# A two-layer decoder on one core: the first group's rows and weight quads ahead of the other groups' rows, and the next group's first quad ahead of its attention

## The chip, the cores and the metric

The kernel runs on one core of a Trainium2 chip, as one launch. The metric is device time in microseconds (us), as the median of several executions. Before the change it is 1839.93 us (three executions, 1838.93 to 1842.21). The engines are named as in the profile: PE is TensorE (matrix products and transposes), PEld its weight loads, DVE is VectorE, ACT is ScalarE, POOL is GpSimd, SP is the engine that issues most of the transfers.

## The reference, cut to what matters

`x` is (16, 128, 256) float32: 16 sequences of 128 rows of width 256. Two layers of three blocks each, every block followed by a residual sum and a layer norm:

```
x = LN(x + causal attention, 16 heads of 64)                     number 0
x = LN(x + 8 dense experts, gated by ctx_512 and itok)            number 1
x = LN(x + 2 shared and 16 routed experts, top 2)                 number 2
x = LN(x + attention with a band of 8, 16 heads of 16)            number 3
x = LN(x + cross attention to ctx_512, 16 heads of 16)            number 4
x = LN(x + 8 GELU experts, weighted by a top-1 gate)              number 5
```

For block 1 the gate of expert e at a key position is the sum over r of `ctx_512` where `itok` equals e. Everything is computed in float32.

## The kernel before, in words

**Tiling.** The 16 sequences form NG = 4 groups of GB = 4 sequences, so a group is 512 rows. Its rows are the tile `x` (128 partitions, 4 x 256), and their transpose is `xT` (128 partitions, 2 x 512), made by `transposed` from eight PE transposes (line 51) and two copies, one on DVE (244) and one on ACT (246).

**Attention 0** (`attention0`, from line 347) walks through four quads of four heads. `load_quad` (87) is four transfers of 256 KB: the columns of W_Q, W_K, W_V and the rows of W_O. The tile has three buffers (pool `attn`). `project_quad(j)` makes qT, kT and v of the quad: for i = 0, 1 two products of 512 columns for q and two for k (`project`, 288), evicted by DVE (361) and by ACT (366), then `values` (298): two PSUM tiles of four products of 256 columns (305), each evicted by a DVE copy (309). All of these, the transposes of x and the output products share the two buffers of the PSUM tag "H". A unit (j, b) is one quad for one of the group's four sequences: scores (382) into the single buffer "S", then `softmax` (313): minimum with the causal mask on DVE (319), maximum on DVE (324), four exponentials on ACT (329), reciprocal on DVE (334), product on POOL (335); two steps later the transposes of the weights (51) with an ACT copy (344), two more steps later the product with v (424) and its eviction zT (431), a step later the output product (391) and its sum into x (264). While the units n = 0 to 11 run, each step also takes one piece of `project_quad(j + 1)`. The group's quad 0 is projected by itself, ahead of its unit 0, and during its last four units and the five steps of draining nothing is projected.

**Gates of block 1.** `gates0` (731) reads `it` and `cx` (lines 734 and 293; one buffer each), makes eight tiles `chose` on DVE (743, four buffers shared with `sums`), sums each over the partitions with a product with ones (752), copies the sums on ACT (757), and stores them to HBM (759). They are read back as `gt` (768). It is called from `tail(0, g)`, after attention 0 of the group.

**Order of the work.** `Weaver.weave` fixes the program order at build time: it takes the pieces of a main stream, of a side stream `dense` and of short streams in turn, by a clock of estimated durations; `yield UNTIL` holds a stream until a time of that clock. The attention blocks of groups 0 and 1 are woven alone, those of groups 2 and 3 with `dense` (blocks 1, 2 and 5 of all groups), by shares of 81 to 150; then blocks 3 and 4 with the rest of `dense` (68 to 150); then the rest of `dense` alone. The framework's scheduler then orders each engine's instructions, which can put an instruction far ahead of its place in the program: the first four `chose` of group 0 stand at the very beginning of DVE's stream. In the trace each of DVE, ACT, POOL and SP runs its instructions in the order of its stream. SP's stream is its queue of transfers, with eight semaphores in turn, so that a transfer is issued only once the eighth before it has landed.

**The prologue.** Lines 106 to 108 issue the rows of group 0, quad 0, and the rows of groups 1 to 3; quads 1 and 2 follow, then `it`, `cx`, and weights of block 1. Four short streams `tail(-1, g)` (line 1008) transpose all groups' rows ahead of the first projection.

Of the kernel before, what the change touches and what calls it, by code (L numbers as in the profile page):

```python
# [14 lines left out]
P = 128  # L15
# [4 lines left out]
NG = NB // GB  # L20
# [7 lines left out]
def kernel(ctx: ExitStack, tc: tile.TileContext, a: dict, out: bass.AP):  # L28
# [15 lines left out]
    def bank(tag):  # L44
        return ps.tile([P, T], F32, tag=tag, name=f"ps{tag}")

    mm = nc.tensor.matmul
# [15 lines left out]
    def load_x(g):  # L63
        x = xp.tile([P, GB, D], F32, tag="x", name="x")
        nc.sync.dma_start(
            out=x, in_=a["x"][g * GB:(g + 1) * GB].rearrange("b p d -> p b d")
        )
        return x

    def load_w(tag, size, name, *parts, bufs=None):  # L70
        w = (ap if tag == "attn" else wp).tile([P, size], F32, tag=tag, name=name, bufs=bufs)
        views, at = [], 0
        for part in parts:
            p_, r, c = part.shape
            v = w[:, at:at + r * c].rearrange("p (r c) -> p r c", r=r)
            nc.sync.dma_start(out=v, in_=part)
            views.append(v)
            at += r * c
        return views
# [7 lines left out]
    def load_quad(j):  # L87

        cols = slice(j * D, (j + 1) * D)
        return load_w(  # L90
            "attn", 2048, f"wquad{j}", a["L0_attn_W_Q"][:, :, cols], a["L0_attn_W_K"][:, :, cols],
            a["L0_attn_W_V"][:, :, cols], a["L0_attn_W_O"][:, 2 * j:2 * j + 2, :],
        )
# [9 lines left out]
            f"wg{t}", a["L0_ffn_wg_r"][:, :, cols], a["L0_ffn_wu_r"][:, :, cols]  # L103
        ) + load_down(f"wd{t}", a["L0_ffn_wd_r"][:, 2 * t - 2:2 * t, :])

    xs = [load_x(0)]
    first_quad = load_quad(0)
    xs += [load_x(g) for g in range(1, NG)]


    ident = cp.tile([P, P], F32, tag="ident", name="ident")
    make_identity(nc, ident)
    ones = cp.tile([P, P], F32, tag="ones", name="ones")
    nc.gpsimd.memset(ones, 1.0)
    mhalf = cp.tile([P, GB], F32, tag="mhalf", name="mhalf")
    nc.gpsimd.memset(mhalf, -0.5)

# [66 lines left out]
    UNTIL = "until"  # L184
# [47 lines left out]
    weaver = Weaver()  # L232
# [52 lines left out]
    def project(pt, w, cols, xT):  # L285

        for c in range(KC):
            mm(pt, lhsT=w[:, c, cols], rhs=xT[:, c, :], start=c == 0, stop=c == KC - 1)  # L288
# [9 lines left out]
    def values(xT, w, k):  # L298

        v = p3.tile([P, GB, D], F32, tag="v", name="v")  # L300
        for b in range(0, GB, 2):
            pv = bank("H").rearrange("p (b f) -> p b f", b=2)
            for i in range(2):
                for c in range(k):
                    mm(  # L305
                        pv[:, i, :], lhsT=xT[:, c, (b + i) * P:(b + i + 1) * P],
                        rhs=w[:, c, :], start=c == 0, stop=c == k - 1,
                    )
            nc.vector.tensor_copy(v[:, b:b + 2, :], pv)
            yield 0.86 * k  # L310
        return v
# [32 lines left out]
        return eT, nc.scalar.copy(eT, pt)  # L344


    def attention0(x, xT, g):
        norm = Norm(x)
        norm.bias(bo0)
        heads = {}  # L350

        def project_quad(j):
            wq, wk, wv, wo = first_quad if g == 0 and j == 0 else load_quad(j)
            qT = p2.tile([P, 2, T], F32, tag="qT", name="qT")
            kT = p2.tile([P, 2, T], F32, tag="kT", name="kT")
            for i in range(2):
                c = 2 * j + i
                cols = slice(i * P, (i + 1) * P)
                pq = bank("H")
                project(pq, wq, cols, xT)  # L360
                nc.vector.tensor_scalar(
                    qT[:, i, :], pq, bq0[:, c:c + 1], 0.125, ALU.add, ALU.mult
                )
                pk = bank("H")
                project(pk, wk, cols, xT)
                nc.scalar.activation(kT[:, i, :], pk, AF.Identity, bias=bk0[:, c:c + 1])
                yield 3.44

            v = yield from values(xT, wv, KC)
            heads[j] = qT, kT, v, wo  # L370

        def scores(j, b):
            qT, kT, _, _ = heads[j]
            at = slice(b * P, (b + 1) * P)
            s = ps.tile([P, 2, T], F32, tag="S", name="psS", bufs=1)[:, :, :D].rearrange(
                "p s (i k) -> p s i k", i=2
            )

            for i in range(2):
                for k in range(2):  # L380
                    rows = slice(64 * k, 64 * k + 64)
                    mm(  # L382
                        s[:, k, i, :], lhsT=qT[rows, i, at], rhs=kT[rows, i, at],
                        start=True, stop=True,
                    )
            return softmax(s, causal)

        def output(j, b, zT):
            po = bank("H")[:, :D]
            for i in range(2):  # L390
                mm(po, lhsT=zT[:, i, :], rhs=heads[j][3][:, i, :], start=i == 0, stop=i == 1)  # L391
            norm.add(b, po, last=j == 3)

        yield from project_quad(0)
        units = [(j, b) for j in range(4) for b in range(GB)]
        e, eT, zT, at = {}, {}, {}, {}
        for n in range(len(units) + 5):
            if n < 16:
                j, b = units[n]
                e[n] = scores(j, b)  # L400
                at["e", n] = weaver.now + 9.0
                yield 0.6
            m = n - 2
            if m in e:
                yield UNTIL, at["e", m]
                eT[m], _ = weights_T(e.pop(m))
                at["t", m] = weaver.now + 2.5
                yield 0.5
            m = n - 5
            if m in zT:  # L410
                yield UNTIL, at["z", m]
                output(*units[m], zT.pop(m))
                yield 0.86
            m = n - 4
            if m in eT:
                j, b = units[m]
                yield UNTIL, at["t", m]

                pz = bank("O")[:, :D].rearrange("p (c q) -> p c q", c=2)
                got = eT.pop(m)  # L420
                for i in range(2):
                    for k in range(2):
                        h = 2 * i + k
                        mm(  # L424
                            pz[64 * k:64 * k + 64, i, :],
                            lhsT=heads[j][2][:, b, 64 * h:64 * h + 64], rhs=got[:, 2 * k + i, :],
                            start=True, stop=True,
                        )
                zT[m] = p3.tile([P, 2, P], F32, tag="z", name="zT")

                nc.vector.tensor_tensor(
                    zT[m], pz, bv0[:, 2 * j:2 * j + 2].unsqueeze(2).to_broadcast([P, 2, P]), ALU.add
                )
                at["z", m] = weaver.now + 2.5
                yield 0.6
            if n < 12:

                j, b = units[n]
                if b == 0:
                    ahead = project_quad(j + 1)  # L440
                yield next(ahead)
                if b == 3:
                    assert next(ahead, None) is None
        assert not e and not eT and not zT
        norm.done()
# [498 lines left out]
        )  # L944


    xTs = [None] * NG
    written = [-1] * NG
    extra = [None] * NG

    def tail(number, g):

        if number >= 0:
            yield UNTIL, weaver.now + 7.0
        xTs[g], last = transposed(xs[g], xTs[g])
        transposed_by[g] = [last]
        yield 0.9
        if number == 0:
            yield from gates0(g)
        elif number in (1, 4):  # L960
            yield UNTIL, weaver.now + 2.5
            extra[g] = yield from (route if number == 1 else gate1)(xTs[g])
        written[g] = number
# [13 lines left out]
    def run(number, g):  # L977

        yield lambda: written[g] == number - 1
        x, xT = xs[g], xTs[g]  # L980
        if number == 0:
            yield from attention0(x, xT, g)
        elif number == 1:
            yield from ensemble0(x, xT, g)
        elif number == 2:
            yield from experts0(x, xT, extra[g])
        elif number == 3:
            yield from attention1(x, xT)
        elif number == 4:
            yield from cross1(x, xT, g)  # L990
        else:
            yield from experts1(x, xT, g, extra[g])
        if number not in (1, 5):
            after(tail(number, g))

    def chain(*layers):
        for layer in layers:
            yield from run(*layer)
# [6 lines left out]


    b2sum = cp.tile([P, D], F32, tag="b2sum", name="b2sum")
    weaver.short += [Stream(tail(-1, g)) for g in range(NG)]
    dense = Stream(chain(
        (1, 0), (1, 1), (2, 0), (2, 1), (1, 2), (1, 3), (2, 2), (2, 3),  # L1010
        (5, 0), (5, 1), (5, 2), (5, 3),
# [76 lines left out]
```

## Time and profile before

| what | value |
|---|---|
| median of 3 executions | 1839.93 us |
| the profiled execution | 1837.82 us |
| its span, first to last instruction | 1836.1 us |
| PE busy in the span | 1757.7 us (96%) |
| DVE, ACT, POOL busy | 1050.7, 731.0, 673.8 us |
| PE idle, 0 to 30 us | 12.7 us |
| ACT table loads | 113, of 1.28 us each |

The span counts from the first to the last instruction of the profiled execution; 1.7 us lie around it. A line of the timeline gives start, length, engine, source line, operation, output and inputs, the number of records, and in brackets the idle time before it with what ended it. A float32 product counts as two records. A line of the stages gives a stretch of time, its length, the busy time of each engine with the number of records, the granted TensorE clock, the share of the DMA engines and GB/s.

### The profile page before, as it was taken

What the parts mean: (1) busy time and instruction counts of PE and PEld (TensorE: products, weight loads), DVE (VectorE), ACT (ScalarE), POOL (GpSimd) and SP (SyncE); (2) the same over time, 40 slices, a digit from 0 to 9 for tenths busy, and PEclk for the clock granted to TensorE, in tenths of its full rate; (3) what the DMA queues carried; (4) which work ended last, traced back from release to release, by engine and by line L of the source; (5) the groups of instructions that cost most, each with busy time, mean ns of one, the idle gap of its engine ahead of it and who ended that gap; (6) DMA issues with size and microseconds to landing.
All of it is one profiled execution on the core that took longest, in us unless ns stands there. A gap on an engine that the chain in (4) does not pass through costs nothing.

```text
span 1836.1 us, 21774 instructions
## 1 busy us (share of the span) xinstructions
PE 1757.7 (96%) x7602; PEld 1068.6 (58%) x7602; DVE 1050.7 (57%) x1927; ACT 731.0 (40%) x2161; POOL 673.8 (37%) x568
## 2 busy tenths in 40 slices
PE   7999999999999999999899999999898999999997
PEld 4655566666566565556556565556554565555664
DVE  3555655677565244676776853356546555645645
ACT  2434312112023452151340544936827548376221
POOL 5231235422131222353432624456554234344222
PEclk9999999999999999999999999999998999999999
DMA  5041223323321324123223214232232121222221
GB/s 170 24 134 46 87 78 126 124 75 122 121 86 46 111 92 138 61 99 111 75 87 98 82 57 121 70 116 97 79 116 75 63 94 65 75 75 84 106 96 51
DMA packets 73404, 166.69 MB, mean 91 GB/s; under 512 B 7000, under 2 KB 38800, under 8 KB 73296
## 3 DMA queue, kind: packets, MB, share of 16 engines
q1 hardware_dynamic: 70464, 150.17, 25.5%
q0 software_dynamic: 2832, 15.15, 2.0%
q8 instruction: 60, 0.98, 0.2%
q14 instruction: 48, 0.39, 0.1%
HBM read 148.32 MB, written 16.97 MB: 90 GB/s over the span
## 4 chain that ended last, share of the span: by engine, by line
PE 74%; DVE 11%; ACT 8%; issue 3%; POOL 2%; DMA 2%; SPq 0%; POOLq 0%; DVEq 0%; ACTq 0%
PE psH L288 33%; PE psM L671 16%; ACT e L329 4%; PE psH L305 4%; PE psM L592 4%; PE psO L51 4%; PE psH L391 3%; DVE cm L663 3%; PE psS L382 2%; PE psS L465 2%; PE psO L424 2%; PE psO L477 2%; DVE nmax L324 1%; PE psH L51 1%; ACT L933 1%
## 5 line engine op out<-in xcount | busy, mean ns | idle before, releaser
L288 PE MATMUL psH<-xT,we 128*128 128x512 f32 x1024 | 488.6, 599 | 5.6 <-ACT h L933 3.6
L335 POOL TENSOR_TENSOR e<-e,inv 128x512 f32<-128x512 f32 (+1 forms) x128 | 190.0, 1484 | 420.2 <-DVE inv L334 376.4
L663 POOL TENSOR_TENSOR cm<-h 128x512 f32<-128x512 f32 x128 | 205.3, 1621 | 356.1 <-DVE h L774 164.6
L671 PE MATMUL psM<-cm,wb 128*128 128x256 f32 x1280 | 313.9, 385 | 2.1 <-DVE acc L681 1.6
L329 ACT ACTIVATE e<-e,nmax 128x128 f32<-128x128 f32 x512 | 198.6, 389 | 258.6 <-DVE nmax L324 258.2
L671 PEld LDWEIGHTS psM<-cm,wb 128*128 128x128 f32 x1280 | 238.5, 190 | 99.3 <-issue 65.4
L288 PEld LDWEIGHTS psH<-xT,we 128*128 128x128 f32 x1024 | 187.4, 190 | 165.9 <-issue 137.1
L663 DVE TENSOR_TENSOR cm<-h 128x512 f32<-128x512 f32 x192 | 219.2, 1165 | 40.3 <-ACT h L933 37.9
L681 DVE TENSOR_TENSOR acc<-psM,acc 128x512 f32<-128x512 f32 x224 | 138.5, 619 | 174.8 <-PE psM L671 174.2
L344 ACT COPY eT<-psO 128x512 f32<-128x512 f32 x192 | 106.7, 586 | 147.2 <-PE psO L51 146.3
L933 ACT ACTIVATE h<-psH,b 128x512 f32<-128x512 f32 x128 | 87.2, 687 | 186.1 <-PE psH L288 169.3
L774 DVE SCALAR_TENSOR_TENSOR h<-psH,gt 128x512 f32<-128x512 f32 x128 | 87.7, 685 | 80.4 <-PE psH L288 80.3
L671 PE MATMUL psM<-h,wb 128*128 128x256 f32 x512 | 124.3, 385 | 0.0
L288 PE MATMUL psH<-xT,wquad 128*128 128x512 f32 x256 | 118.7, 606 | 4.6 <-DMA wquad<-in_L_attn_W_Q 1.6
L671 PEld LDWEIGHTS psM<-h,wb 128*128 128x128 f32 x512 | 96.5, 192 | 32.8 <-issue 18.7
L288 PE MATMUL psH<-xT,wg 128*128 128x512 f32 x256 | 115.5, 594 | 0.0
L51 PEld LDWEIGHTS psO<-ident,e 128*128 128x128 f32 x768 | 87.3, 141 | 48.4 <-issue 29.5
L51 PE MATMUL psO<-ident,e 128*128 128x128 f32 x768 | 112.5, 280 | 1.7 <-POOL e L335 0.9
L329 ACT ACTIVATE e<-psS,nmax 128x128 f32<-128x128 f32 x256 | 89.9, 377 | 38.4 <-DVE nmax L324 35.4
L329 ACT ACTIVATION_READ_ACCUMULATOR e<-e,nmax 128x1 f32 x512 | 95.7, 187 | 0.0
L457 POOL TENSOR_TENSOR kb<-kT,hm 128x512 f32<-128x512 f32 x64 | 70.1, 1097 | 69.2 <-PE psS L465 33.2
L879 POOL TENSOR_TENSOR hT<-sg,cw 128x512 f32<-128x512 f32 x32 | 41.4, 1292 | 130.6 <-DVE sg L878 130.6
(173 smaller groups left out, 2243.8 us busy)
## 6 DMA issues: line engine op xcount, KB each, us to landing
wb<-wbd SPq DMA_DIRECT2D x48, 896.0 KB
we<-in_L_xattn_proj_in SPq DMA_DIRECT2D x32, 512.0 KB
we<-in_L_ffn_w SPq DMA_DIRECT2D x32, 512.0 KB
wbd<-wb POOLq DMA_DIRECT2D x16, 896.0 KB, 6.0
gt<-gatesd SPq DMA_DIRECT2D x32, 256.0 KB
cw<-combd SPq DMA_DIRECT2D x64, 128.0 KB
wquad<-in_L_attn_W_Q SPq DMA_DIRECT2D x16, 256.0 KB
wquad<-in_L_attn_W_K SPq DMA_DIRECT2D x16, 256.0 KB
```

Source lines behind the costliest of these rows:

```text
L51: return nc.tensor.transpose(out_, in_, ident[:n, :n])
L288: mm(pt, lhsT=w[:, c, cols], rhs=xT[:, c, :], start=c == 0, stop=c == KC - 1)
L305: mm(pv[:, i, :], lhsT=xT[:, c, (b + i) * P:(b + i + 1) * P], rhs=w[:, c, :], start=c == 0, stop=c == k - 1,)
L329: nc.scalar.activation(e[:, h, :], s[:, h // (n // 2), h % (n // 2), :], AF.Exp, bias=nmax[:, h:h + 1], accum_out=total[:, h:h + 1],)
L335: nc.gpsimd.tensor_tensor(e, e, inv.unsqueeze(2).to_broadcast([P, n, P]), ALU.mult)
L344: return eT, nc.scalar.copy(eT, pt)
L592: step = mm(acc[b], lhsT=held[:, b * P:(b + 1) * P], rhs=down(i), start=i == 0 and b % 2 == 0, stop=i == n - 1, skip_group_check=True,)
L663: engine.tensor_tensor(t[:, s % 2], half(e, one), half(e, two), op)
L671: step = mm(pm[:, s % 2, :], lhsT=blocks[e][:, s, q, :], rhs=parts[e, s][:, q, :], start=q == 0 and s % 2 == 0, stop=q == 1, skip_group_ch ...
L681: nc.vector.tensor_tensor(to, pm[:, :len(slots), :], to, ALU.add)
L774: nc.vector.scalar_tensor_tensor(out=h, in0=ph, scalar=0.0, in1=up[1], op0=ALU.max, op1=ALU.mult)
L933: nc.scalar.activation(h, ph, AF.Gelu, bias=b1[:, 4 * e + c:4 * e + c + 1])
```

## The change

- The rows of group 0 are followed by quads 0 and 1. The rows of groups 1 to 3 are issued by a new stream `begin(g)`, at 20 g us of the weaver's clock, and transposed ten of its microseconds later.
- Nine products of a tile of ones with itself are put on PE ahead of everything else.
- `project_quad` takes the group as well; during units 12 to 15 of groups 0, 1 and 2 it projects quad 0 of the next group, which then skips its own first projection. The table `heads0` is shared by the groups.

In the streams as built, SP's transfers up to `cx` are the same 18 (22 times 256 KB), in the order x0, quad 0, quad 1, x1, quad 2, x2, x3, it, cx. On DVE the first `chose` stands ahead of the first copy of v, and two more ahead of the second. The transposes of groups 1, 2 and 3 stand in group 0's attention, at units 5, 10 and 14. ACT has 105 table loads.

```diff
-    xs = [load_x(0)]
-    first_quad = load_quad(0)
-    xs += [load_x(g) for g in range(1, NG)]
+    xs = [load_x(0)] + [None] * (NG - 1)
+    first_quads = [load_quad(j) for j in range(2)]
...
     nc.gpsimd.memset(ones, 1.0)
+
+    pw = bank("M")
+    for _ in range(9):
+        mm(pw[:, :P], lhsT=ones, rhs=ones, start=True, stop=True)
...
-    def attention0(x, xT, g):
+    xTs = [None] * NG
+    heads0 = {}
+
+    def attention0(x, g):
         norm = Norm(x)
         norm.bias(bo0)
-        heads = {}
-
-        def project_quad(j):
-            wq, wk, wv, wo = first_quad if g == 0 and j == 0 else load_quad(j)
+
+        def project_quad(g, j):
+            wq, wk, wv, wo = first_quads[j] if g == 0 and j < 2 else load_quad(j)
+            xT = xTs[g]
...
             v = yield from values(xT, wv, KC)
-            heads[j] = qT, kT, v, wo
+            heads0[g, j] = qT, kT, v, wo
...
-        yield from project_quad(0)
+        if (g, 0) not in heads0:
+            yield from project_quad(g, 0)
...
-            if n < 12:
+            if n < 16 and (n < 12 or g + 1 < NG):
 
                 j, b = units[n]
                 if b == 0:
-                    ahead = project_quad(j + 1)
+                    ahead = project_quad(g, j + 1) if j < 3 else project_quad(g + 1, 0)
                 yield next(ahead)
...
-    weaver.short += [Stream(tail(-1, g)) for g in range(NG)]
+    def begin(g):
+
+        if g > 0:
+            yield UNTIL, 20.0 * g
+            xs[g] = load_x(g)
+            yield UNTIL, 20.0 * g + 10.0
+        yield from tail(-1, g)
+
+    weaver.short += [Stream(begin(g)) for g in range(NG)]
```

More of the change, by code (lines that the diff above doesn't have):

```diff
@@ L369, in project_quad @@
             v = yield from values(xT, wv, KC)
-            heads[j] = qT, kT, v, wo
+            heads0[g, j] = qT, kT, v, wo
         def scores(j, b):
-            qT, kT, _, _ = heads[j]
+            qT, kT, _, _ = heads0[g, j]
             at = slice(b * P, (b + 1) * P)
@@ L390, in output @@
             for i in range(2):
-                mm(po, lhsT=zT[:, i, :], rhs=heads[j][3][:, i, :], start=i == 0, stop=i == 1)
+                mm(po, lhsT=zT[:, i, :], rhs=heads0[g, j][3][:, i, :], start=i == 0, stop=i == 1)
             norm.add(b, po, last=j == 3)
-        yield from project_quad(0)
+        if (g, 0) not in heads0:
+            yield from project_quad(g, 0)
         units = [(j, b) for j in range(4) for b in range(GB)]
@@ L425, in attention0 @@
                             pz[64 * k:64 * k + 64, i, :],
-                            lhsT=heads[j][2][:, b, 64 * h:64 * h + 64], rhs=got[:, 2 * k + i, :],
+                            lhsT=heads0[g, j][2][:, b, 64 * h:64 * h + 64], rhs=got[:, 2 * k + i, :],
                             start=True, stop=True,
@@ L944, in experts1 @@
         )
-    xTs = [None] * NG
     written = [-1] * NG
@@ L981, in run @@
         if number == 0:
-            yield from attention0(x, xT, g)
+            yield from attention0(x, g)
         elif number == 1:
```

## Prediction

> **What bounds the kernel now.** I read the page first: busy shares and the chain that ended last.
>
> ```profile
> PE 1757.7 (96%) x7602; PEld 1068.6 (58%) x7602; DVE 1050.7 (57%) x1927; ACT 731.0 (40%) x2161; POOL 673.8 (37%) x568
> ...
> PE 74%; DVE 11%; ACT 8%; issue 3%; POOL 2%; DMA 2%; SPq 0%; POOLq 0%; DVEq 0%; ACTq 0%
> ```
>
> PE is the bound; all that can be won is its idle time, 1836.1 - 1757.7 = 78.4 us. The change works in the first 230 us, so I asked next for the stages there (columns: stretch, length, busy PE, PEld, DVE, ACT, POOL, granted clock, DMA share, GB/s):
>
> ```profile
> 18.05:31.25 13.20, 11.42 (x40) 6.43 (x40) 5.13 (x8) 1.65 (x3) 9.32 (x8) 1.00 0.69 231
> 31.25:71.00 39.75, 39.75 (x238) 24.91 (x236) 24.36 (x48) 22.27 (x84) 9.57 (x11) 1.00 0.03 10
> 98.67:126.71 28.04, 25.67 (x126) 15.54 (x125) 14.04 (x35) 6.31 (x21) 4.80 (x6) 1.00 0.37 118
> 126.71:150.00 23.29, 18.74 (x98) 10.14 (x98) 14.73 (x24) 9.64 (x35) 9.93 (x12) 0.93 0.38 119
> 200.00:229.50 29.50, 27.05 (x126) 14.12 (x124) 17.42 (x39) 5.09 (x14) 6.57 (x5) 1.00 0.32 99
> ```
>
> From 31 to 71 us PE has no idle time at all: what is moved in there costs its full length. Idle: 2.37 us where group 0 drains and group 1 starts, 4.55 in the stage of the gates, 2.45 from group 1 to 2. Then the timeline of DVE and PE at the two places where DVE holds PE up:
>
> ```profile
> 25.55 0.69 DVE L743 SCALAR_TENSOR_TENSOR chose<-it,cx 128x512 f32<-128x512 int32 x1 [4.73 <-DMA cx<-in_ctx]
> ...
> 143.21 0.69 DVE L743 SCALAR_TENSOR_TENSOR chose<-it,cx 128x512 f32<-128x512 int32 x1 [4.19 <-DMA cx<-in_ctx]
> ```
>
> ```profile
> 14.16 1.94 PE L51 MATMUL psH<-ident,x 128*128 128x128 f32 x8 [0.23 <-DMA x<-in_x]
> 16.63 1.07 PE L51 MATMUL psH<-ident,x 128*128 128x128 f32 x8 [0.53 <-DMA x<-in_x]
> 18.05 7.13 PE L288 MATMUL psH<-xT,wquad 128*128 128x512 f32 x16 [0.35 <-DVE xT L244]
> 26.96 3.72 PE L305 MATMUL psH<-wquad,xT 128*128 128x256 f32 x16 [1.78 <-DVE qT L361]
> ...
> 31.25 3.70 PE L288 MATMUL psH<-xT,wquad 128*128 128x512 f32 x8
> ...
> 144.62 0.71 PE L382 MATMUL psS<-kT,qT 64*128 64x128 f32 x8 [3.37 <-DVE e L319]
> ...
> 146.81 4.97 PE L288 MATMUL psH<-xT,wquad 128*128 128x512 f32 x8
> ```
>
> A `chose` of DVE waits for the transfer of `cx`, and what stands behind it in DVE's stream waits too: the second qT (26.16), so PE's products for v.
>
> **What the Trainium skill says.** "TensorE: Matmul & The Clock Gate", Part 1: a TensorE idle for a window of about 3.4 us falls to half clock and needs about as much activity to come back. The trace agrees: eight transposes take 1.94 us at 14.16 and 1.07 at 16.63; after the idle 3.37 us eight records take 4.97 in place of 3.70. The same page, Part 4, has it that transposes don't count as activity; here they warmed the array by 16.63, before any product. The same page, "Architectural detail", calls VectorE's queue a strict FIFO; the 4.73 us at 25.55, with a qT ready behind it, agree. "DMA: Bandwidth & Descriptors", section "Queues, rings and completion order": each DMA engine takes descriptors in ring order. So `cx` lands after what is issued ahead of it, whatever the order of that.
>
> **The change, part by part.**
>
> *1. The first projection moves forward, but cx does not.* x0 landed at 5.09; with 1.94 us of transposes, copies to 7.64 and 7.13 us of projection, PE ends quad 0's q and k near 15.3, v (3.72) near 19.0, scores at 19.7. The next product, q of quad 1, needs the bank of the first half of v. Its copy stands on DVE behind the first `chose`. `cx` is the 18th transfer, behind the same 5.5 MB as before, in a stretch where the DMA engines are 93% busy; I take 25.55 again (bounds 24.5 and 26.5). `chose` to 26.24, copy of v to 26.9: PE goes on there, where before it did at 31.25, 4.3 us earlier. It has been idle for over 7 us, so it resumes cold: 3.4 to 5 us at half clock lose 1.3 (as at 146.81) to 2.5; I take 1.9. Gain 2.4.
>
> *2. The nine products of ones.* They and the earlier start lie wholly ahead of 26.9, hidden behind the wait for `cx`: nothing either way. If that cover were gone, warm transposes would save 0.9 us (1.94 - 1.07).
>
> *3. 24 transposes leave the prologue*, where PE waited for rows anyway, for the full stretch from 31 us on. One group's eight displaced 0.53 + 0.58 us at 118.78 to 120.32: 3 x 1.1 = 3.3 us lost. Their two copies (0.69, 0.59) fit in DVE and ACT; three bias sums on POOL (9.26 / 4 = 2.3 us each) stand between weight products that have a step of slack. Parts 1 and 3: 0.9 us lost.
>
> *4. The next group's quad ahead.* At the end of group 0 the built stream has group 1's scores between the last output products, and quad 1's projection directly behind. Of the idle 2.37 us I leave 0.5 (the last zT, 0.53 at 107.26): gain 1.9. From group 1 to 2, of 2.45 leave 0.65: gain 1.8. From 2 to 3 the dense stream covers it already: 0. The price: the tile of the quad is released by the output products of unit n = 12, and the transfer must land at once. The same wait at quad 3 cost 0.35 us at 71.07 and 0.85 at 172 to 175; three more of them, with one covered by dense: 1.0 lost (0 to 2).
>
> *5. The gates' stage.* Count from the first product of the gates, T0 (126.71 before). SP: before, the stores of the sums waited 3.6 us behind a weight transfer (`we`, 131.63), gt was issued 3.9 us after the stores, `it` and `cx` at 137.41 and 138.17, and `cx` landed 5 us later, T0 + 16.5. In the built order `we` stands behind `cx`, so the stores come at T0 + 2, gt at 6, `cx` at 8.2, landing at 12.6 to 13.4. PE has work until T0 + 14.9: gates 2.1, four transposes of weights, v, scores, the projection's first half, an output, a q. Then k of the second half needs a bank that DVE's sum into x frees, behind `chose`, `chose`, e, `chose`, nmax and the sum: 4 x 0.69 + 0.67 + 0.4 = 3.8 us after landing, T0 + 16.4 to 17.2. Idle 1.5 to 2.3 us plus small ones, in place of 4.55 and the 1.27 of cold clock: gain 2.7 (bounds 0 and 4.5).
>
> *6. Later.* Quad 0 of group 2 leaves the stage that is woven with dense, so dense stands 11 us x 150/81 = 20 us later against the main stream from there on. The stream has 105 ACT table loads for 113, 8 x 1.28 = 10 us less of ACT, of which I put a tenth on the path: gain 1.0. The new neighbourhoods of the rest can cost or give some 3 us.
>
> **Sum**, against the profiled span: -2.4 + 3.3 - 1.9 - 1.8 + 1.0 - 2.7 - 1.0 = -5.5, 1836.1 to 1830.6, with the 1.7 us around it 1832.3. The profiled execution (1837.82) stood 2.1 under the median of 1839.93; so the median goes to 1834.4.
>
> **Rivals.**
>
> *Nothing to measure.* The wait for the second `cx` stays as long as before (a landing at T0 + 16.5 would put PE's return beyond T0 + 17.9, where it was), and only boundaries and transposes are left, which nearly cancel. For it: DVE's longer queue ahead of the bank's release; against it: `we` is out of the way on SP. Without part 5, and with 1.3 for part 6's neighbourhoods, 1834.4 + 2.7 + 1.3 = 1838.4.
>
> *Slower: ACT in layer 1.* From 1140 to 1500 us PE is idle for 17.2 us, in stretches where ACT switches between Exp and GELU tables and is full (19.82 of 20 us at 1300 to 1320). Moving dense by 20 us rearranges this. If eight more of the 1.28 us loads came to lie on the path there, in place of one less, PE would lose 10.2 us: 1834.4 + 10.2 = 1844.6. It decides once the exposed loads there grow by more than 7, which eats 9.2 us (5.5 and the 3.7 of the bound). Against it: for the two functions the built stream has 34 + 46 loads, before 35 + 50.
>
> *Far faster.* If `cx` landed 8 us earlier, quad 1 would follow quad 0 at once and part 1 would give some 10 us more: 1824. Against it: the chain shows W_K of quad 1 landing at 18.17 and `cx`, eight transfers of 256 KB later, at 25.55, which is 285 GB/s; at that rate the 5.5 MB alone take 19 us from their start.
>
> That the change doesn't do what it says is excluded by the built order, which I compared.
>
> **Numbers.** Forecast 0.60 (own range 1831.5 to 1837.5), nothing 0.22, slower 0.13, far faster 0.05. 0.2% is 3.7 us, about what a measurement of this kernel can tell from no change. Of the forecast 0.47 lies under 1836.2, 0.13 above; of "nothing" 0.02 under, 0.18 within, 0.02 above. Faster 0.54, same 0.31, slower 0.15. Range 1827 to 1842: it takes in the bounds of parts 1, 4, 5 and 6 and leaves out the far faster case and the worse two thirds of the slower one.
>
> **What would show it.** PE idle from about 19 to 27 us, ended by DVE's copy of v, DVE waiting until 25 or 26 for `cx`; products at half speed after it. Quad 1's k ended near 32.5 (before 34.95). Idle at the drains under 1 us. In the gates' stage one PE wait of about 2 us, ended by DVE's sum into x. PE busy within 3 us of 1757.7, its idle time 5 us less. I would be wrong if `cx` lands well before 24, if PE waits over 4 us in the gates' stage, or if idle from 1140 on changes by more than 4 us.

## The result, and the profile after

| kernel | median | against before (95%) |
|---|---|---|
| before, beside it | 1837.65 us (13 executions) | |
| changed | 1842.45 us (13 executions, 1839.51 to 1847.49) | 1.0028 (1.0020 to 1.0037) |

The change costs about 5 us; the forecast was a gain of 5.5. The medians below come from several series of executions, each with the kernel before beside it, and a ratio is against that one. The page of the changed kernel (busy time of each engine; the chain that ended last, by engine):

```profile
span 1840.9 us, 21821 instructions
...
PE 1768.8 (96%) x7620; PEld 1071.2 (58%) x7620; DVE 1046.8 (57%) x1927; ACT 721.7 (39%) x2153; POOL 674.1 (37%) x568
...
PE 77%; DVE 9%; ACT 7%; DMA 2%; issue 2%; POOL 1%; SPq 0%; POOLq 0%; DVEq 0%; ACTq 0%
```

PE's idle time fell, from 78.4 to 72.1 us, and the kernel is slower all the same: PE is busy 11.1 us longer. The ones are 4.0 of that; the other 7.1 are the same 7602 records taking longer. DVE and ACT have less to do than before. A page's sums don't say where the time went. So I gave each kind of PE record one length (0.43 us for 512 columns, 0.22 for 256, 0.13 for a transpose, and so on, from the groups of the page), added them up in the order of the built stream without the ones, and read from the timeline when each amount of work was reached. The difference to before is a kernel's lead (below zero) or lag at that point, in us:

| before is at | 46.7 | 161 | 269 | 707 | 1135 | 1271 | 1444 | 1591 | end |
|---|---|---|---|---|---|---|---|---|---|
| changed | -1.1 | -8.7 | -6.0 | -6.1 | -7.7 | +5.7 | -1.4 | +5.1 | +4.8 |

The early part does what was forecast of it, with a lead of 6.0 us after the boundary of groups 1 and 2. It is lost in layer 1, in two parts: 13.4 us where before goes from 1135 to 1271 (1127 to 1277 on the clock of the changed kernel), of which 7.1 come back by 1444, and 6.5 more by 1591. (Such a table is of one profiled execution. It shows the place of a loss better than its size: the profiled executions of e3 and e4 below ran 3.7 and 2.8 us over the medians of their kernels, and small differences between the rows can be the execution's. The lengths given to the records are a choice too; another such choice moves an entry by up to about 1 us.)

The early part in the timeline of the changed kernel, DVE and then PE (start, length, operation, idle time before it and what ended that):

```profile
24.05 0.69 DVE L750 SCALAR_TENSOR_TENSOR chose<-it,cx 128x512 f32<-128x512 int32 x1 [11.44 <-DMA cx<-in_ctx]
24.66 0.68 DVE L312 COPY v<-psH 128x512 f32<-128x512 f32 x1
...
143.65 1.30 DVE L750 SCALAR_TENSOR_TENSOR chose<-it,cx 128x512 f32<-128x512 int32 x2 [2.11 <-DMA cx<-in_ctx]
```

```profile
1.21 3.98 PE L117 MATMUL psM<-ones 128*128 128x128 f32 x18 [1.21 <-POOL ones L113]
5.03 1.04 PE L51 MATMUL psH<-ident,x 128*128 128x128 f32 x8
6.41 7.13 PE L291 MATMUL psH<-xT,wquad 128*128 128x512 f32 x16 [0.35 <-DVE xT L247]
...
25.40 5.33 PE L291 MATMUL psH<-xT,wquad 128*128 128x512 f32 x8 [7.76 <-DVE v L312]
...
164.93 5.40 PE L291 MATMUL psH<-xT,wquad 128*128 128x512 f32 x8 [1.40 <-DMA wquad<-in_L_attn_W_Q]
```

DVE stands 11.44 us for `cx`, with the copy of v behind the `chose`, and PE waits 7.76 us for that copy and resumes cold: the granted clock is at half from 21.9 to 28.7 us, and eight records take 5.33 us in place of 3.70. In the stage of the gates DVE waits 2.11 us for the second `cx`, and PE doesn't wait at all: from 117.6 to 163.5 us its records follow each other without a gap.

The late part. Two stretches, before and then changed (columns as in the stages of the prediction):

```profile
1220.00:1240.00 20.00, 18.86 (x71) 10.05 (x70) 15.16 (x38) 11.65 (x16) 12.68 (x14) 1.00 0.45 157
1240.00:1260.00 20.00, 18.66 (x71) 12.67 (x68) 12.75 (x16) 15.03 (x40) 11.64 (x8) 1.00 0.11 40
```

```profile
1220.00:1240.00 20.00, 15.62 (x54) 8.79 (x53) 12.65 (x24) 5.77 (x16) 12.49 (x16) 0.93 0.56 171
1240.00:1260.00 20.00, 20.00 (x58) 10.00 (x57) 10.82 (x13) 17.99 (x50) 11.50 (x8) 0.90 0.08 27
```

PE is idle for 4.4 us in the first and then "busy" at a granted clock of 0.90: 112 records in 40 us where before did 142. The records differ in kind; by the lengths given to them the two stretches hold some 29 us of work against 37. What held PE is seen on POOL. First before, then changed (L629 to L637 of before are L636 to L644 of changed: the second building of a weight block of block 5 in each kernel, seven sums and copies from the weights `raw` as they landed into the block `wb`, and its store to HBM):

```profile
1222.03 1.41 POOL L631 TENSOR_TENSOR wb<-raw 128x256 f32<-128x256 f32 x2 [4.98 <-PE psM L592]
1223.38 0.74 POOL L629 COPY wb<-raw 128x256 f32<-128x256 f32 x2
1224.08 2.08 POOL L631 TENSOR_TENSOR wb<-raw 128x256 f32<-128x256 f32 x3
...
1227.13 1.05 POOL L278 TENSOR_TENSOR rstd<-ve,mhalf 128x4 f32<-128x4 f32 x1
```

```profile
1227.55 1.41 POOL L638 TENSOR_TENSOR wb<-raw 128x256 f32<-128x256 f32 x2 [4.41 <-DMA raw<-in_L_ffn_w]
1228.90 0.73 POOL L636 COPY wb<-raw 128x256 f32<-128x256 f32 x2
1229.61 2.08 POOL L638 TENSOR_TENSOR wb<-raw 128x256 f32<-128x256 f32 x3
1231.98 0.59 POOL L644 DMA_DIRECT2D wbd<-wb  x1 [0.30 <-POOL wb L638]
1232.60 1.04 POOL L281 TENSOR_TENSOR rstd<-ve,mhalf 128x4 f32<-128x4 f32 x1
```

DVE of the changed kernel:

```profile
1227.56 0.74 DVE L279 TENSOR_SCALAR ve<-mv 128x4 f32<-128x4 f32 x1
...
1233.68 3.10 DVE L283 TENSOR_SCALAR x<-x,mv,rstd 128x256 f32<-128x256 f32 x4 [4.26 <-POOL rstd L281]
```

PE at this place, before and then changed:

```profile
1231.41 1.13 PE L465 MATMUL psS<-kb,qT 64*128 64x512 f32 x4
1232.87 0.65 PE L51 MATMUL psH<-ident,x 128*128 128x128 f32 x4 [0.33 <-DVE xT L244]
1234.05 1.98 PE L288 MATMUL psH<-xT,wa 128*128 128x512 f32 x4 [0.53 <-ACT h L933]
```

```profile
1235.95 2.07 PE L51 MATMUL psH<-ident,x 128*128 128x128 f32 x8 [3.22 <-DVE x L283]
1239.18 2.04 PE L472 MATMUL psS<-kb,qT 64*128 64x512 f32 x2 [1.16 <-DVE e L322]
1241.15 3.31 PE L291 MATMUL psH<-xT,we 128*128 128x512 f32 x4
```

In both kernels a layer norm's `rstd` (the reciprocal root of its variance `ve`) stands behind a block's building on POOL. Before, the building was nearly over when `ve` started (1226.14 us). In the changed kernel `ve` starts at 1227.56 and ends at 1228.3, when the building, which waited 4.41 us for its weights `raw`, has just begun: rstd follows 4.3 us later, then 3.10 us of DVE, and PE, out of work, waits 3.22 us and runs cold after it: the granted clock is at half from 1237.0 to 1243.8 us (transposes 2.07 for 1.07, four records 3.31 for 1.98). Not all of that cold time is this wait's: e7 below doesn't have the wait, and its clock is at half from 1236.4 to 1239.8 us.

### The profile page after: what moved, and what is told of

Read it like the earlier page. It is cut to its first block, busy times and chain, and to the rows that moved or that the text cites. A ratio compares the mean times of both kernels' runs of the same rounds, so it can differ in the third digit from the quotient of the medians.

```text
span 1840.9 us, 21821 instructions
## 1 busy us (share of the span) xinstructions
PE 1768.8 (96%) x7620; PEld 1071.2 (58%) x7620; DVE 1046.8 (57%) x1927; ACT 721.7 (39%) x2153; POOL 674.1 (37%) x568
## 4 chain that ended last, share of the span: by engine, by line
PE 77%; DVE 9%; ACT 7%; DMA 2%; issue 2%; POOL 1%; SPq 0%; POOLq 0%; DVEq 0%; ACTq 0%
PE psH L291 34%; PE psM L678 18%; PE psH L308 4%; ACT e L332 4%; PE psO L51 3%; PE psM L599 3%; PE psH L397 3%; PE psS L472 2%; DVE cm L670 2%; PE psS L388 2%; PE psO L431 2%; DVE nmax L327 2%; PE psO L484 1%; PE psH L51 1%; PE psH L508 1%
## 5 line engine op out<-in xcount | busy, mean ns | idle before, releaser
L670 DVE TENSOR_TENSOR cm<-h 128x512 f32<-128x512 f32 x192 | 226.5, 1199 | 47.4 <-ACT h L940 45.1
L678 PEld LDWEIGHTS psM<-h,wb 128*128 128x128 f32 x512 | 94.7, 190 | 30.7 <-issue 16.7
L472 PE MATMUL psS<-kb,qT 64*128 64x512 f32 x256 | 81.8, 651 | 12.2 <-ACT e L332 7.8
```

The costliest lines, as they stand in the source:

```text
L472: mm(s[:, k, :], lhsT=qT[rows, c, at], rhs=kb[rows].rearrange("p h k -> p (h k)"), start=True, stop=True,)
L670: engine.tensor_tensor(t[:, s % 2], half(e, one), half(e, two), op)
L678: step = mm(pm[:, s % 2, :], lhsT=blocks[e][:, s, q, :], rhs=parts[e, s][:, q, :], start=q == 0 and s % 2 == 0, stop=q == 1, skip_group_ch ...
```

## The experiments

Theory A: parts 1 to 5 of the prediction hold; the loss comes from what step 6 dismissed, the dense stream's new place against the main stream. Rivals: B, every re-plan is a lottery and no trend of the lag; C, a direct part of the change costs. All runs but e2 and e8 start from the changed kernel; a diff shows what a run adds to the kernel that its heading names.

**e1: the woven stage's shares set back so that dense isn't later.**

```diff
-    weaver.weave(Stream(chain((0, 2), (0, 3))), dense, (81.0, 150.0))
+    weaver.weave(Stream(chain((0, 2), (0, 3))), dense, (75.6, 150.0))
```

> The changed kernel with the stage of groups 2 and 3 woven by shares of 75.6 to 150 in place of 81 to 150, so that the dense stream is as far at the end of that stage as in the kernel before, though the main stream holds one quad less. Theory A (the loss comes from the dense stream standing some 20 us later against the main stream): the early lead of 11 to 12 us by 200 us stays, the loss of 16 us between 1190 and 1290 us mostly goes, 1827 to 1833 us, against 1837.7 before and 1842.4 changed. Rival B (any re-plan of the later order is a lottery; the loss is one collision, not the lag): the lead stays, the end lies anywhere from 1827 to 1843. Rival C (a direct part of the change costs, and the later loss is its consequence): 1841 to 1844, as the changed kernel.

Measured 1836.21 us, 0.9988 (0.9981 to 0.9994).

**e2: the kernel before with dense set 20 us later, nothing else.** `(81.0, 150.0)` becomes `(86.8, 150.0)`.

> The kernel before with shares of 86.8 to 150 in that stage, so that its dense stream is set back by about 20 us and nothing else of the change is done. Theory A: equal to before up to 120 us, then a loss of 10 to 16 us in layer 1, 1846 to 1852 us. Rival B: 1833 to 1846, with the loss or gain at other places. Rival C: within 2 us of 1837.7.

Measured 1847.16 us, 1.0044 (1.0032 to 1.0057).

**e3: no projection ahead from group 1 to 2.**

```diff
-            if n < 16 and (n < 12 or g + 1 < NG):
+            if n < 16 and (n < 12 or g in (0, 2)):
```

> The changed kernel without the projection ahead from group 1 to group 2 (quad 0 of group 2 stays in the woven stage; from 0 to 1 and from 2 to 3 it is ahead as changed). The main stream of the woven stage is then as long as before, so the dense stream is not set back. Theory A: lead of 9 to 10 us (the idle of about 2 us at that boundary is back), late loss gone, 1828 to 1834 us. Rival B: 1828 to 1844. Rival C: 1840 to 1844.

Measured 1835.71 us, 0.9981 (0.9974 to 0.9988).

**e4: no projection ahead at all.** The same line becomes `if n < 12:`.

> The changed kernel without any projection ahead: the order of the first rows and quads, the later rows of groups 1 to 3 and the products of ones stay. Theory A: lead of 6 to 7 us at 100 us, some 2 us less after the boundary of groups 0 and 1, no gain in the stage of the gates, dense as before, 1831 to 1835 us. Rival B: 1829 to 1844. Rival C: if the prologue is the part that costs, 1840 or more; if the projection ahead costs, 1831 to 1835 as well.

Measured 1840.18 us, 1.0006 (0.9998 to 1.0014).

| before is at | 46.7 | 161 | 269 | 707 | 1135 | 1271 | 1444 | 1591 | end |
|---|---|---|---|---|---|---|---|---|---|
| e1 | +1.5 | -5.3 | -5.8 | -2.0 | -2.8 | -1.5 | -3.2 | -1.4 | -1.5 |
| e2 | -1.0 | -1.0 | -1.8 | -3.5 | -4.7 | +8.8 | +1.8 | +8.3 | +7.9 |
| e3 | +1.1 | -6.0 | -3.9 | +1.3 | +1.4 | +1.4 | +1.4 | +1.4 | +1.6 |
| e4 | +1.2 | +2.0 | +1.8 | +2.2 | +4.9 | +4.9 | +3.2 | +4.9 | +5.0 |

By the ranges that stood on record only e2 speaks for A. e1 and e3 lie 3.2 and 1.7 us above A's range and inside B's, and e4's 1840.18 lies in those of B and C. A's ranges for e1, e3 and e4 reckoned with an early lead of 6 to 12 us, and the table shows less. The orders of PE's records in the traces explain the pattern better than these ranges: from a point in the woven stage on, e3 has the order of the kernel before, word for word (from 528 us), e1 too (from 701 us), and e2 has that of the changed kernel (from 682 us). e2, which contains nothing of the change but the lag, has the same losses at the same places:

```profile
1230.75 1.41 POOL L631 TENSOR_TENSOR wb<-raw 128x256 f32<-128x256 f32 x2 [4.61 <-DMA raw<-in_L_ffn_w]
...
1235.81 1.05 POOL L278 TENSOR_TENSOR rstd<-ve,mhalf 128x4 f32<-128x4 f32 x1
```

```profile
1239.17 2.21 PE L51 MATMUL psH<-ident,x 128*128 128x128 f32 x8 [3.42 <-DVE x L280]
```

So by the ratios the new order from the woven stage on costs 8.1 us by itself (e2 against before) or 7.4 (changed against e1), and C falls as the cause of the late loss. e4, the prologue's part alone, costs 1.1 us (-0.4 to 2.6); e3 against e4 gives the projection ahead without that from 1 to 2: 4.6 us gained.

**e5: is the wait for cx (part 1) worth what it shows?** The first `chose` of group 0 is tied behind the copy of its transposes after attention 0.

```diff
+                if g == 0 and q == 0 and r == 0:
+                    together(step, *transposed_by[g])
```

> The changed kernel with the first chose of group 0 tied to the copy of group 0's transposes after attention 0, so that DVE no longer waits for cx at 17 to 24 us with the copy of v behind it. The later order of PE stays nearly word for word that of the changed kernel. If part 1 of the prediction names the right wait (DVE's copy of v behind chose), PE's idle of 7.8 us before quad 1 and the cold products after it go: 6 to 9 us less by 40 us, 1834 to 1837 us against 1842.4. Rival: the wait only changes its name (the transfers of quad 1, or of x1, or the first scores' eviction, are late as well), under 2 us gained, 1840.5 to 1843 us.

Measured 1842.20 us, 1.0023 (1.0013 to 1.0033): the rival. The wait had only stood in front of another. POOL and then PE:

```profile
28.02 0.72 POOL L638 TENSOR_TENSOR wb<-raw 128x256 f32<-128x256 f32 x1 [11.87 <-DMA raw<-in_L_xattn_proj_out]
28.68 0.74 POOL L636 COPY wb<-raw 128x256 f32<-128x256 f32 x2
29.39 2.08 POOL L638 TENSOR_TENSOR wb<-raw 128x256 f32<-128x256 f32 x3
31.43 2.03 POOL L338 TENSOR_TENSOR e<-e,inv 128x512 f32<-128x512 f32 x2
```

```profile
25.28 0.71 PE L388 MATMUL psS<-kT,qT 64*128 64x128 f32 x8
32.52 1.12 PE L51 MATMUL psO<-ident,e 128*128 128x128 f32 x4 [6.53 <-POOL e L338]
```

Quad 1 now follows at once, but a weight block's building, scheduled some 200 us before PE first uses a block (240 us in the changed kernel), waits 11.87 us for its `raw` and holds the first two softmax products `e` behind it. It is the mechanism of 1232 us, at 28.

**e6: e3 and e5 together.**

> The kernel of the third run (nothing projected ahead from group 1 to 2, so the late order is that of the kernel before; 1835.7 us) with the first chose of group 0 tied to the copy after attention 0 as well. If both causes are right and independent (the wait for cx at the start, the dense stream's lag later), their gains add: 1835.7 - 6 to 9 = 1827 to 1830 us, faster than both kernels. Rival (the cx wait is replaced by another): 1834 to 1836 us.

Measured 1834.78 us, 0.9978 (0.9971 to 0.9985): the rival again, for the same reason.

**e7, e8: the changed kernel and the kernel before without the building of layer 1's blocks.**

```diff
+        if layer == 1:
+            got, = load_down("wb", in_hbm[0, e])
+            return got.rearrange("p s (q d) -> p s q d", q=2)
         raw, = load_up("raw", w)
```

> The changed kernel without the building of layer 1's weight blocks: the first use of an expert in block 5 reads the blocks of layer 0 from HBM instead of loading layer 1's and summing them on POOL. So the second experts' down projection uses other weights. To be read against its twin, the kernel before with the same left out. Theory A1 (the late loss is POOL's rstd standing behind a weight build that waits for its transfer, with what follows from it at 1216 to 1260 us): PE's wait of 3.2 us at 1236 and its cold products go, and the changed kernel is no longer slower than its twin, difference -3 to 0 us. Rival A2 (the loss is ACT's: exponentials, GELU and their table loads meet at other places): the difference stays at 4 to 6 us.

> The twin: the kernel before without the building of layer 1's weight blocks, which reads the blocks of layer 0 instead. Both theories expect little here against 1838.7, since no wait over 1.4 us lies at its first block 5: 1834 to 1839 us. It is the base for the run above: A1 expects it within 3 us above that run, A2 expects it 4 to 6 us under that run.

Measured: e7 1831.25 us, 0.9961 (0.9947 to 0.9975); e8 1841.51 us, 1.0017 (1.0008 to 1.0027). The changed kernel was 4.8 us slower; without the building it is 10.3 us faster than its twin, beyond A1's 0 to 3. (e8 lost some 3 us by dropping work, above its range of 1834 to 1839, which neither theory expected.) From 1135 us to the end the lead changes by +3.8 us in e7 and +3.3 in e8, where with the building it was +12.5 against 0. The norm of e7:

```profile
1226.94 1.01 POOL L281 TENSOR_TENSOR rstd<-ve,mhalf 128x4 f32<-128x4 f32 x1 [5.53 <-DVE ve L279]
```

```profile
1232.32 0.66 PE L51 MATMUL psH<-ident,x 128*128 128x128 f32 x4
```

rstd waits for nothing but its `ve`, and PE's transposes of x follow without idle time. PE's order in e7 is that of the changed kernel but for eleven small moves between 1234 and 1272 us, so the two can be compared place by place. By the same reckoning e7 leads by 9 us where before is at 1135, 3 at 1271, 11 at 1444, 5 at 1591 and 6 at the end. From 1135 to 1271 it loses 6 us where the changed kernel loses 13; from 1271 on the two move alike. So 7 to 8 us of the late loss hang on the building of block 5's weights on POOL, about 5 of them right after the norm (1236 to 1260) and 3 near 1270 us, where a sum `cm` of DVE takes 6.52 us (last section), 6.51 in e2, and none in e7 takes over 1.9 between 1230 and 1300. The other 6 us there stay without the building, and so do the 6 between 1444 and 1591: in that stretch PE has the same waits, 7.8 us in all, in the changed kernel, e2 and e7 (on DVE's `acc` and `zT` and ACT's `h` for the most part), where before has 2.1. That part belongs to the order itself.

**e9: e6 with the first block's building tied too.** Until then only its first sum was tied; the other six had been scheduled ahead.

```diff
-            if s == 0:
+            if s == 0 or (layer, e) == (0, 0):
                 together(step, *transposed_by[g])
```

> The kernel of the sixth run (no quad ahead from group 1 to 2, the first chose late; 1834.8 us), with all seven sums of the very first weight block of layer 0 tied to the copy of group 0's transposes after attention 0, where one was before. In the profile of the fifth run POOL stood 11.9 us for the transfer of raw, with the products e of the first softmax behind it, so PE's idle of 7.8 us before quad 1 had only turned into 6.5 us before the first transposes of weights. Theory: with both out of the way PE runs on from quad 1, 5 to 8 us gained by 45 us, 1827 to 1830 us. Rival: a third wait takes their place (transfers of quad 1 or 2, or the copy of group 1's rows), 1833 to 1836 us.

Measured 1829.74 us, 0.9962 (0.9948 to 0.9976). Where before is at 46.7 us it leads by 10.1. But at the gates the same thing waits again (POOL, then PE):

```profile
129.76 1.40 POOL L638 TENSOR_TENSOR wb<-raw 128x256 f32<-128x256 f32 x2 [3.20 <-DMA raw<-in_L_xattn_proj_out]
131.11 0.73 POOL L636 COPY wb<-raw 128x256 f32<-128x256 f32 x2
131.81 1.03 POOL L338 TENSOR_TENSOR e<-e,inv 128x512 f32<-128x512 f32 x1
```

```profile
132.89 1.12 PE L51 MATMUL psO<-ident,e 128*128 128x128 f32 x4 [3.77 <-POOL e L338]
```

**e10: without the ones.** The three lines of `pw` are left out.

> The changed kernel without the nine products of ones; every other instruction of every engine stays in its place. Prediction's part 2: they are hidden behind the wait for cx, within 1 us of the changed kernel, 1841.5 to 1843.5 us. Rival: the ones warm the clock for the first projection and that counts, 1844 to 1846 us; or they cost, 1838 to 1841 us.

Measured 1844.08 us, 1.0035 (1.0022 to 1.0047). The profiled execution begins cold (transposes 1.94, first projection 9.30 us for 7.13) and is 2.2 us behind the changed kernel at 45 us, 0.5 at 220, and 0.3 ahead at the end. The intervals overlap: nothing is shown either way.

**e11, e12: the start of e9 with all of the change, at 75.6 and at 78 to 150.**

> The kernel of the first run (all of the change, the woven stage at 75.6 to 150, late order as before; 1836.2 us) with the first chose and the first weight block tied as in the run above. If the start is worth 6 to 8 us whatever follows: 1828 to 1830.5 us, faster than both kernels. Rival, as above: 1834 to 1837 us.

> The same with 78 to 150, halfway between 75.6 and 81, so that the dense stream stands some 10 us later against the main stream in place of 0 or 20. Theory A in its strict form (loss grows with the lag): 1831 to 1834 us, between the run above and that run plus 8. Rival B (each lag makes its own collisions in layer 1, a lottery without a trend): outside of that, anywhere from 1824 to 1840 us.

Measured: e11 1834.24 us, 0.9980 (0.9973 to 0.9987), the rival, and only 2 us under e1: in its profile the lead of 10 us at 46.7 has shrunk to 3 where before is at 1135. e12 1849.84 us, 1.0069 (1.0055 to 1.0083), is the worst of all, at half the lag, and worse than the range of B too (1824 to 1840). Theory A in its strict form falls.

**e13: e9 with the first two blocks tied to group 1's copies.**

```diff
-            if s == 0 or (layer, e) == (0, 0):
-                together(step, *transposed_by[g])
+            if (layer, e) in ((0, 0), (0, 1)):
+                together(step, *transposed_by[1])
+            elif s == 0:
+                together(step, *transposed_by[g])
```

> The kernel of the ninth run (1829.7 us) with the first two weight blocks of layer 0 tied to copies of group 1's transposes in place of group 0's. In the profile of the ninth run POOL waits 3.2 us at 129.76 for the transfer of raw of the second block, with a softmax product e behind it, and PE waits 3.77 us for that e at 132.89 and goes on cold. Theory (a POOL build that waits for raw holds whatever stands behind it, wherever it falls): that idle goes, 3 to 6 us gained, 1824 to 1827 us. PE's stream is the same word for word. Rival: the first block, now at about 47 us in the full stretch, holds products e there for 6.5 us of building, and PE pays it: 1829 to 1832 us.

Measured 1827.15 us, 0.9951 (0.9939 to 0.9963): the lowest median here, faster than both kernels, though its interval and that of e9 overlap. Where before is at 161 us it leads by 17.3, e9 by 10.3: the wait of 3.77 us and the cold records after it (half clock from 132.0 to 138.8 us in e9) were worth 7. Of its lead 3.6 us go back by 269 us (PE's waits for DVE's qT there grow from 1.2 to 3.3 us).

**e14, e15: two more places of dense, 73 and 84 to 150, with the start of e9. e16: e12 without the building of layer 1's blocks.**

> The kernel of the eleventh run with shares of 73 to 150: the dense stream some 10 us ahead of where it is in the kernel before. Theory A strict (loss grows with the lag, so less than no lag gains or is level): 1830 to 1834.5 us, not above the eleventh run (1834.2). Rival B (every relative position makes its own collisions, no trend; the twelfth run at half the lag, 1849.8, was worse than the full lag): anything from 1826 to 1848, and above 1836 would show it once more.

> The same with 84 to 150: the dense stream some 30 us later than in the kernel before. Theory A strict: later than with 81, so above 1842, 1843 to 1852 us. Rival B: anything from 1826 to 1848; below 1838 would end theory A.

> The kernel of the twelfth run (78 to 150, 1849.8 us) without the building of layer 1's weight blocks, as in the seventh and eighth: the first use of an expert in block 5 reads layer 0's blocks from HBM, so the second experts' down projection uses other weights. If POOL's builds are the general cause of what a re-planned order loses, it falls below 1838 us. Rival: at this position other collisions lose the time (in the twelfth run's profile DVE's h of block 1 and xT from 695 to 1133 us, 10 us more than before, ahead of the first layer 1 build), so it stays above 1843 us.

Measured: e14 1841.31 us, 1.0022 (1.0009 to 1.0034); e15 1838.10, 1.0005 (0.9995 to 1.0015); e16 1831.14, 0.9974 (0.9961 to 0.9987). With one start, the shares 73, 75.6, 78 and 84 give 1841.3, 1834.2, 1849.8 and 1838.1 us: no trend, and a spread of 15.6 us. That is what rival B says. e12's leads against e16's:

| before is at | 46.7 | 269 | 707 | 1135 | 1271 | 1444 | 1591 | end |
|---|---|---|---|---|---|---|---|---|
| e12 | -10.2 | -10.7 | -11.7 | -2.0 | +1.8 | +9.3 | +13.5 | +11.1 |
| e16 | -9.8 | -11.3 | -12.4 | -3.8 | -2.3 | -8.2 | -4.0 | -6.7 |

Both theories of e16 named a part: the loss of 9 us between 707 and 1135 us stays, ahead of any building of layer 1, and the 13.1 us lost from there to the end turn into 2.9 gained. So at this place the late loss goes with the building, and the earlier one doesn't. (PE's order in e16 is that of e12 but for ten small moves between 1365 and 1406 us.)

## Why the prediction was wrong, point by point

- **Parts 1 and 3** (-2.4 and +3.3, 0.9 us lost): not contradicted. e4 does these two and the ones alone: 1.1 us lost, within its interval, and +1.2 where before is at 46.7. The landing of `cx`, taken as 25.55 (bounds 24.5 and 26.5), was 24.05 in the profile of the changed kernel, under the bound, but 25.79, 25.68 and 25.58 in e1, e3 and e4 with the same first transfers. So quad 1's k ended at 30.7 where 32.5 was forecast, and near 33 in those. *"Far faster"* (1824) was priced as a landing 8 us earlier. e5 shows that this alone is not enough: the building on POOL was next in line. The timeline of POOL before has it already; the prediction reads DVE and PE alone:

```profile
28.05 1.25 POOL L631 TENSOR_TENSOR wb<-raw 128x256 f32<-128x256 f32 x1 [3.88 <-DMA raw<-in_L_xattn_proj_out]
29.24 0.73 POOL L629 COPY wb<-raw 128x256 f32<-128x256 f32 x2
29.95 2.09 POOL L631 TENSOR_TENSOR wb<-raw 128x256 f32<-128x256 f32 x3
34.76 1.04 POOL L335 TENSOR_TENSOR e<-e,inv 128x512 f32<-128x512 f32 x1 [2.72 <-DVE inv L334]
```

  There it stood free, 2.7 us ahead of the first e. With both out of the way (e9) the start is worth the 10 us that this rival gave it. (Its sum against itself mixes units: 22 times 256 KB are 5.77 million bytes, 20 us at 285 GB/s and not 19.)
- **Part 2** (0): not contradicted; e10 can't tell 0 from 1 us.
- **Parts 4 and 5.** From 0 to 1 (1.9) and at the gates (2.7), less two thirds of the quad waits' 1.0, the sum was 3.9; e3 against e4 measures 4.6. In the profiles e3 gains 7.1 us between 46.7 and 161. The gates were under-sized: the part's own numbers leave 3.5 to 4.3 us (4.55 and 1.27, less 1.5 to 2.3), and 2.7 was taken for small idle times that it doesn't list. `cx` landed 12.4 us after the first product of the gates, just ahead of the forecast 12.6 to 13.4, and PE, with a quad more in hand, had no idle time where 1.5 to 2.3 was forecast. The quad waits were under-sized too: after one of them (1.40 us at 164.93) the granted clock was at half from 165.2 to 168.6 us, and eight records took 5.40 us for 3.70. That makes 3.1 us for this one where 1.0 was put for three; the prediction had reckoned with cold records after idle times of 3.4 us and more alone.
- **Part 6 is the step that failed.** It has dense "20 us later against the main stream", and then the price was "gain 1.0", with "some 3 us" either way for new neighbourhoods. That re-plan costs 7.4 to 8.1 us (e1, e2): in the late stretch POOL's buildings of weights stand ahead of the norm's rstd and beside DVE's sums (7 to 8 us, e7), and the new order has waits of its own on DVE and ACT (e7 again); some of the loss comes back between them. The sum up to there, -4.5, stands against a lead of 6.0 in the profile.
- **"All that can be won is its idle time."** That reading of the page is too narrow, and the signs that hang on it mislead. PE's idle time was to be 5 us less and is 6.3 less, but that is luck: 4.0 of it are the ones, which fill an idle stretch. Its busy time was to stay within 3 us and grew by 11.1, for records at half clock count as busy. The last sign, idle time from 1140 on changing by more than 4 us, came true: it grew by 9.0.
- **The rival that came true in sign and size** (1844.6, "ACT in layer 1") named the right stretch and the wrong engine. Of PE's idle time from 1140 us on (25.4 us before, 34.4 changed) the part that ends on ACT grew by 3.2 (10.4 to 13.6), the part that ends on DVE by 9.1 (10.7 to 19.8). The rival's mechanism, more table loads on the path, has nothing to stand on: between 1140 and 1500 us the traces have 52 loads before and 46 changed. Two of the longest, 3.22 us for x and 2.96 for cm, end on DVE and come from POOL, which the list of PE's waits names for 1.0 us in all. So its 1844.6 was near by luck. It had 13% of the chances; the range, 1827 to 1842, ended 0.45 us under the result. (The 2.1 us that the prediction adds to get from the profile to the median rest on three executions: thirteen have their median at 1837.65, level with the profiled 1837.82.)
- **What would have been seen beforehand:** not the collision itself, but its size. Before has 17.2 us of idle time between 1140 and 1500 us, much of it where main and dense streams meet. When every meeting there is dealt anew, a spread of the order of that idle time fits better than 3 us; the four shares of e11, e12, e14 and e15 spread over 15.6. That is an estimate from this one kernel and no bound: a new order can add waits that the old one didn't have.

What stays open: which of the building's effects (the wait for `raw`, POOL's time, its transfers on SP's queue) makes each later loss; e7 and e16 take all of them away at once, and they move a few of PE's records as well. Tying only rstd ahead of the building, or loading `raw` into a buffer of its own, wasn't tried. Open too is what makes the 6 us between 1444 and 1591, and the 9 us of e12 between 707 and 1135.

## What to carry to other kernels

A change that moves a planned stream moves every later meeting of the streams; price that as its own term, sized by the idle time of the stretches where they meet, and test it by moving the plan alone, without the change (here e2, one constant). When the part that fails is far from the edit, compare positions at equal work, not busy time: here PE's idle time fell and the kernel was slower. And a wait seen in front of an in-order engine may cover another: before counting its removal as a gain, ask of every other engine what it would wait for at that moment, here a building on POOL that the scheduler had put 100 to 200 us ahead of its need.

## What the runs showed of the hardware

Two sums `cm` of DVE took 7.12 us in the changed kernel, while POOL worked through an `e`, two `cm` and two `kb` beside it. Nearly all of it is the first one, 6.52 us, to 1275.72; the second took 0.68, and so did the next, after POOL had finished:

```profile
1269.19 7.12 DVE L670 TENSOR_TENSOR cm<-h 128x512 f32<-128x512 f32 x2 [1.26 <-ACT h L940]
1276.24 0.68 DVE L688 TENSOR_TENSOR acc<-psM,acc 128x512 f32<-128x512 f32 x1
1276.84 0.68 DVE L670 TENSOR_TENSOR cm<-h 128x512 f32<-128x512 f32 x1
```

```profile
1268.83 1.91 POOL L338 TENSOR_TENSOR e<-e,inv 128x1024 f32<-128x1024 f32 x1
1270.69 2.49 POOL L670 TENSOR_TENSOR cm<-h 128x512 f32<-128x512 f32 x2
1273.14 2.02 POOL L464 TENSOR_TENSOR kb<-kT,hm 128x512 f32<-128x512 f32 x2
```

PE waited 2.96 us for the first. The Trainium skill has it so ("SBUF — State Buffer", section "SBUF: two separate sides"): a DVE operation with two SBUF inputs and a GpSimd operation share one pair of ports, which the one that starts first holds for the whole instruction. The trace agrees: POOL's five instructions lie back to back from 1268.83 to 1275.16, and DVE's first sum, begun at 1269.19, ends 0.56 us after them; it got in between none of the five. So POOL's work can be dearer than its 37% of busy time suggests.

With the ones, eight transposes at 5 us took 1.04 us and the first projection 7.13; without them (e10) 1.94 and 9.30. In the changed kernel the clock was at half after an idle time of 1.40 us (165.2 to 168.6 us) as after one of 3.22 (from 1237.0), and in e7 after idle times of 0.45 and 0.83 us (1236.4 to 1239.8).
